# Attention and mixture of experts on one core: a chunk's residual put off by half a slot, and the layernormed inputs of q and k taken amid the next scores

## The chip, the cores and the metric

The kernel runs on one core of a Trainium2 chip. The metric is the device time of the whole program in microseconds (us), shorter is better. A core has a matrix engine (TensorE, "PE"), a vector engine (VectorE, "DVE"), a scalar engine for activation functions (ScalarE, "ACT"), a general one (GpSimd, "POOL") and an engine that issues transfers (SyncE, "SP"). Each works through its own list of instructions, and semaphores order them against each other. Matrix products land in PSUM, an accumulator memory; everything else lives in SBUF, the memory on the core, or in DRAM.

## The reference

The input x has 8 batches of 1024 tokens with 512 features, in 32 bit floating point. Two sublayers follow each other, each with a layernorm before it and a residual sum around it.

```
h   = layernorm(x)
q, k: cos and sin (by a table of 2048 steps) of  h / (1+|w|) + b + t * phi      # t: the token's place
v   = cos + sin of                               h / (1+|w_v|) + b_v
out = softmax(causal(q k^T / sqrt(2*32))) v        # 16 heads of 32 features
x   = x + (cos + sin of out / (1+|w_out|) + b_out)
h   = layernorm(x)
p   = softmax(h Wr + br);  the two best of 8 experts; at most 160 tokens of a batch per expert
x   = x + sum over the two of  p * (relu(h W1[e] + b1[e]) W2[e] + b2[e])
```

The angle formulas work on 16 heads of 32 features. The experts have 2048 hidden features.

## The kernel before, in words

**Slots.** The 512 features of a batch are cut into 4 chunks of 128 features (4 heads). One chunk of one batch is a *slot*, so there are 32 slots, n = 0 to 31, with b, c = divmod(n, 4). The main loop (L1209 on) does one slot per turn, and each turn mixes work of several chunks: scores and value products of chunk n, the rest of the value products and the output of chunk n-1, the angles of chunk n+1 and n+2, and the router of the batch before. After the loop come the experts (`experts`), which the change leaves alone.

**A slot in two halves.** A chunk's four heads make two pairs. `scores` (L584) yields one step at a time. A step multiplies keys with queries for a block of at most 512 queries (L602, with a causal mask added by L616) into a PSUM tile `ps_s`, and ScalarE takes the exponential (L622). A pair has ten steps. `attend` (L627) multiplies the exponentials with v into a tile `av` (L636), and its last step copies that to SBUF as `av_sb` on VectorE (L644). The first half of a slot has the ten steps of pair 0, and the second those of pair 1. `some(k, gen)` takes k steps of a generator, and `rest(gen)` all that are left. `with_asides(k)` (inside the loop) takes k score steps of pair 0, and after each step one step of every generator in `asides`: `v_pre` (three steps of VectorE work for v), one of batch b+1's `layernorm1` halves in some slots, and in slots with c = 2 the router's choice.

**q and k.** `qk_pre(m)` transposes the layernormed input of chunk m on TensorE (16 matmuls, L202) into one `ps_s` tile, and four VectorE instructions (L495) turn it into angles in `qk_f`, adding a table from `qk_base`. `angle` (L426) shifts these into `qk_r`. ScalarE then squares `qk_f` (L430, in two parts) and takes absolute values of `qk_r` into `qk_c` (L509, in two parts): this is `qk_abs`. In the middle of the next slot `qk_sin` takes both sines, and `qk_post` multiplies (L436) and copies the results by eight transfers each (L527) into the next chunk's two `qk` tiles, from `qk_c` first and from `qk_r` second. `qk_f`, `qk_r`, `qk_c` and `qk_base` exist once each, so `angle` may write `qk_r` only when the transfers out of it have landed. `load_base` fetches the next 1 MB table.

**Output and residual.** In slot n `turn` transposes the values of chunk n-1, divides, and `o_pre` makes the output's angle. After the sine and the square `o_post` (L567) does the residual: a product (L436 on `t_r`), a sum into `x_mid` (L576), and eight statistics for the second layernorm (L579). `x_mid` holds one batch of x; `load_mid` fetches it (2 MB, L374) in the slot with c = 1, when the router has read the old one.

**The router** of batch b-1 (`router`, L688) is a generator that runs through slots of batch b. It starts in the second half of the slot with c = 0 (variable `begin`): statistics, an inverse root, and the first two token tiles normalised (L706) and stored. In the slot with c = 1 it takes eight steps at points called `route_on(1)`: four times `features` (transpose two token tiles into a `ps_s` tile, copy them on VectorE to `xT`, L733, and normalise the next two) and, after each, `sums` (product with the router's weights, L767, and a copy, L772). In the slot with c = 2 `sums` ends and the choice of experts follows (L804 to L835).

**Order.** TensorE, VectorE and ScalarE execute in the order in which this program writes their instructions: a manual schedule (`tc.manual_schedule`). Only the queues of SyncE and GpSimd are ordered by the planner of the framework. The planner also decides which free buffer of a pool a tile gets. `ps_s` has three buffers, `av` two, `t_r` and `o_p` two.

The second half of a slot, before the change, in its core:

```
some(2, *ahead)                    # score steps of pair 1
begin = c == 0 and late            # late: not the first slot
if begin:   rest(residual); route = router(b - 1); next(route)
elif ...:   qk_st = rest(qk_pre(n + 2))
next(residual)                     # product and sum of the residual
angle(*qk_st)                      # unless begin
rest(residual)                     # the eight statistics
route_on(1)                        # c == 1: features, the copy L733
```

Of the kernel before, what the change touches and what calls it, by code (L numbers as in the profile page):

```python
# [73 lines left out]
def preln_attn_moe_kernel(  # L74
# [120 lines left out]
    def two_banks():  # L195
        return ps_sc.tile([P, 2, 512], F32, name="ps_s")

    def by_halves(turned, src):

        for a in range(2):  # L200
            r = slice(a * 64, (a + 1) * 64)
            nc.tensor.transpose(turned[:, a, :], src[r, :], ident[r, r])  # L202
# [222 lines left out]
    def angle(p, r):  # L425
        nc.vector.tensor_scalar(r, p, TURN_SHIFT, None, ALU.logical_shift_left)  # L426

    def square(p):
        f = p.bitcast(U16).rearrange("p (s two) -> p s two", two=2)[:, :, 0]
        nc.scalar.activation(p.bitcast(F32), f, AF.Square, bias=split_c, scale=1.0 / FINE)  # L430

    def sine(r):
        nc.scalar.activation(r.bitcast(F32), r, AF.Sin, scale=STEP_ACT)

    def times(out, f, s):
        nc.vector.scalar_tensor_tensor(out, f.bitcast(F32), LIFT, s, ALU.add, ALU.mult)  # L436
# [34 lines left out]
    def load_base(n):  # L471
        if 1 < n < NCH:
            rest(make_base(n))
            return
        p = qkt.tile([P, 2, S], F32, name="qk_base")
        nc.sync.dma_start(p, base_d[n % NCH])
        bases[n] = p

    def qk_pre(n):

        b, c = divmod(n, NCH)
        base = bases.pop(n)
        p = qkt.tile([P, 2, S], I32, name="qk_f")
        r = qkt.tile([P, 2, S], I32, name="qk_r")
        ps = two_banks()
        for t in range(NTT):
            by_halves(
                ps[:, :, t * 64 : (t + 1) * 64],
                xn_tiles[b][t // 4][:, t % 4, c * P : (c + 1) * P],
            )  # L490

        for i in range(2):
            for a in range(2):
                cols = lambda t: t[:, i, :].rearrange("p (t a q) -> p t a q", a=2, q=64)[:, :, a, :]
                nc.vector.scalar_tensor_tensor(  # L495
                    cols(p), ps[:, a, :].rearrange("p (t q) -> p t q", q=64),
                    inv_qk[:, i * NCH + c : i * NCH + c + 1], cols(base), ALU.mult, ALU.add,
                )
            yield p, r

    def qk_abs(st):

        f, r = st
        for i in range(2):
            square(f[:, i, :])
            yield
        c = qkt.tile([P, 2, S], F32, name="qk_c")
        for i in range(2):
            nc.scalar.activation(c[:, i, :], r[:, i, :], AF.Abs)  # L509
            yield c, f, r  # L510

    def qk_sin(st):
        c, f, r = st
        nc.scalar.activation(c, c, AF.Sin, bias=quarter_c, scale=-STEP_ACT)
        sine(r)

    def qk_post(st):
# [36 lines left out]
    def heads(t):  # L554
        return t.rearrange("p (t a d) -> p t a d", a=HPC, d=DH)

    def v_post(n, st):
        times(v_tiles[n % 2][:, :, :, :DH], heads(st[0]), heads(st[1].bitcast(F32)))
# [89 lines left out]
    def some(count, *gens):  # L648

        for gen in gens:  # L650
            while count and next(gen, 0) is None:
                count -= 1

    def rest(gen):
        got = None
        for got in gen:
            pass
        return got
# [207 lines left out]
    def part(gen):  # L866

        for name in gen:
            if name is not None:
                return  # L870
            yield

    def keep(box, gen):
        for box[0] in gen:
            yield
# [302 lines left out]
    NCK = B * NCH  # L1178
# [6 lines left out]
    qk_st = rest(qk_pre(0))  # L1185
    angle(*qk_st)
    rest(base1)
    mask()
    v_st = rest(v_pre(0))
    qk_st = rest(qk_abs(qk_st))  # L1190
    qk_sin(qk_st)
    pairs = rest(qk_post(qk_st))
    sine(v_st[1])
    square(v_st[0])
# [2 lines left out]
    load_base(1)  # L1197
    last = None
    o_st = route = first_rows = None
    place, angles = [None], iter(())  # L1200
    for n in range(NCK):
        more, late = n + 1 < NCK, last is not None
        b, c = divmod(n, NCH)
        if n == NCK - 1:
            to_inputs.close()
            first_rows = experts_begin()
        pos_n = trig.tile([P, S], F32, name="o_p")
        if late:
            e11, halves1, pos = last  # L1209
        es, halves = [[], []], [[], []]  # L1210

        products = [attend(n, 0, h, es[h], halves[0]) for h in range(2)]
        if late:
            products.insert(0, attend(n - 1, 1, 1, e11, halves1))
        ahead = [scores(pairs[0], h, es[h]) for h in range(2)]
        v_box = [None]
        asides = [keep(v_box, v_pre(n + 1))] if more else [first_rows]
        if b == 0 and c in (1, 2):  # L1220
            asides.append(layernorm1(1, c - 1))
        elif c == 0 and b + 1 < B:
            asides.append(layernorm1(b + 1, 1))
        elif c == 3 and b + 2 < B:
            asides.append(layernorm1(b + 2, 0))
        def route_on(slot):
            if c == slot and route is not None:
                next(route)

        def with_asides(count):  # L1230
            for _ in range(count):
                some(1, *ahead)
                for g in asides:
                    next(g, None)


        if late:
            some(3, *products)
        route_on(1)
        route_on(2)  # L1240
        if c == 2 and route is not None:
            asides.append(part(route))
        if n == 0:
            with_asides(3)
            qk_st = rest(qk_pre(1))
            angle(*qk_st)
            angles = keep(place, qk_abs(qk_st))
            with_asides(2)
        else:
            with_asides(5)  # L1250
        route_on(1)
        route_on(1)
        rest(angles)
        if more:
            v_st = v_box[0]
            square(v_st[0])
        if late:
            some(4, *products)
        route_on(1)
        with_asides(5)  # L1260
        for g in asides:
            rest(g)
        if n == 1:
            load_mid(0)
        if late:
            turn(1, halves1, pos)
            o_st = o_pre(n - 1, pos)
        route_on(1)
        if c == 1 and b > 0:
            load_mid(b)  # L1270
        if n == 2:
            load_b1()
        if c == 2 and b + 2 < B:
            load_x(b + 2)
        if c == 3 and b > 0:
            next(route)
            if b > 1:
                fetch_slots(b - 2)
            scatter()


        some(3, *products)
        if more:
            qk_st = place[0]
            qk_sin(qk_st)
            sine(v_st[1])
        if late:
            sine(o_st[1])
        if more:
            post = qk_post(qk_st)  # L1290
            next(post)
        some(NTT, *products)
        if n == 0:
            load_base(2)


        es, halves1 = [[], []], []
        ahead = [scores(pairs[1], h, es[h]) for h in range(2)]
        route_on(1)
        route_on(2)  # L1300
        some(2, *ahead)
        turn(0, halves[0], pos_n)
        next_pairs = rest(post) if more else None
        some(1, *ahead)
        if late:
            square(o_st[0])
            residual = o_post(n - 1, o_st)
        some(2, *ahead)
        begin = c == 0 and late
        if begin:  # L1310

            rest(residual)
            route = router(b - 1)
            next(route)
        elif n + 2 < NCK:
            qk_st = rest(qk_pre(n + 2))
        if late:
            next(residual, None)
        if n + 2 < NCK and not begin:
            angle(*qk_st)  # L1320
        if late:
            rest(residual)
        route_on(1)
        if more and not begin:
            v_post(n + 1, v_st)
        some(3, attend(n, 1, 0, es[0], halves1))
        route_on(1)
        some(5, *ahead)
        if n + 2 < NCK:
            if begin:  # L1330
                qk_st = rest(qk_pre(n + 2))
                angle(*qk_st)
            angles = keep(place, qk_abs(qk_st))
            if not begin:
                some(2, angles)
        if more and begin:
            v_post(n + 1, v_st)
        if n + 3 < NCK:
            load_base(n + 3)
        last = (es[1], halves1, pos_n)  # L1340
        pairs = next_pairs
    rest(attend(NCK - 1, 1, 1, es[1], halves1))
# [54 lines left out]
```

## Time and profile before

| what | value |
|---|---|
| time, median of 3 runs | 3413.85 us (3410.76 to 3418.34) |
| the profiled execution's own time | 3403.52 us |
| span of that execution's profile | 3401.6 us |
| mean granted TensorE clock | 0.982 |
| TensorE busy | 3205.5 us (94%) |
| VectorE busy | 2285.9 us (67%) |
| ScalarE busy | 1320.5 us (39%) |
| first score matmul | 51.85 us |
| slot 17 (batch 4, chunk 1), first score matmul to that of slot 18 | 747.70 to 805.52 us |
| slot 18 (batch 4, chunk 2) | 805.52 to 841.75 us |

The span runs from the first to the last instruction; what lies around it makes the execution's own time. A line of the timeline has the start in us from the span's start, the duration, the engine, the line of the program, the operation, the tiles written and read, their sizes, how many instructions were merged, and in brackets how long the engine was idle just before and who ended that wait. A line of the waits has who waited, for whom, the sum of the waits, how often, and the longest. A wait is put down to the engine whose signal came last.

### The profile page before, as it was taken

How to read it: one execution, taken by the hardware profiler on the slowest of the kernel's cores; microseconds unless marked ns; L12 is line 12 of the kernel's file. 1: busy time of each engine (PE TensorE's matmuls, PEld its weight loads, DVE VectorE, ACT ScalarE, POOL GpSimd, SP SyncE). 2: the span in 40 equal slices, each digit the busy share in tenths (PEclk: the TensorE clock that was granted, in tenths of full speed). 3: DMA queues.
4: the chain of work that ended last, by engine and by line, in shares of the span. 5: the costliest groups of instructions: out<-in, count | busy, mean ns of one | idle time of the engine just before them, and what ended most of it. 6: DMA issues, size and time to landing. Idle time of an engine off the chain costs nothing.

```text
span 3401.6 us, 48876 instructions
## 1 busy us (share of the span) xinstructions
PE 3205.5 (94%) x18942; PEld 2173.0 (64%) x18942; DVE 2285.9 (67%) x5064; ACT 1320.5 (39%) x1609; POOL 417.8 (12%) x363
## 2 busy tenths in 40 slices
PE   3998989898989898899999999999999999999998
PEld 1444444444444444468778778788688688688687
DVE  7886868686868676656566656756747746845844
ACT  5787878787868786311111111101101101201201
POOL 1000202020202021330100110111011011011010
PEclk9999999999999999999999999999999999999999
DMA  4444444444444344232312322322313322323221
GB/s 145 141 123 135 124 137 113 137 119 131 137 137 119 106 132 106 75 97 65 106 50 65 106 48 68 105 44 72 106 38 78 105 36 76 108 43 87 88 41 25
DMA packets 233967, 320.79 MB, mean 94 GB/s; under 512 B 21528, under 2 KB 154376, under 8 KB 221320
## 3 DMA queue, kind: packets, MB, share of 16 engines
q1 hardware_dynamic: 211120, 275.47, 27.6%
q0 software_dynamic: 22528, 42.18, 7.0%
q8 instruction: 150, 2.46, 0.3%
q14 instruction: 81, 0.66, 0.1%
q10 hardware_dynamic: 88, 0.02, 0.0%
HBM read 188.67 MB, written 61.82 MB: 74 GB/s over the span
## 4 chain that ended last, share of the span: by engine, by line
PE 57%; DVE 3%; DMA 1%; issue 1%; ACT 0%; POOL 0%; POOLq 0%; SPq 0%; DVEq 0%; ACTq 0%
PE ps_p L1070 28%; PE ps_p L1025 25%; PE av L636 1%; PE ps_s L602 1%; PE ps_t L981 1%; DMA slot_d<-token,slot 0%; DMA xn_d<-xn 0%; DMA out_dram<-y,slots 0%; DMA xg<-xn_d,source 0%; DMA qk<-qk_r 0%; DVE t L1010 0%; DVE t L1009 0%; ACT hid L1057 0%; DVE hid L1053 0%; DVE y L1086 0%
## 5 line engine op out<-in xcount | busy, mean ns | idle before, releaser
L622 ACT ACTIVATE e<-ps_s 128x1024 f32<-128x1024 f32 (+1 forms) x640 | 569.3, 937 | 299.2 <-PE ps_s L602 202.8
L602 PE MATMUL ps_s<-qk 64*128 64x512 f32 (+3 forms) x3072 | 605.7, 513 | 55.4 <-DMA qk<-qk_r 21.4
L1070 PE MATMUL ps_p<-w,hid 128*128 128x256 f32 x2560 | 569.9, 380 | 0.0
L1070 PEld LDWEIGHTS ps_p<-w,hid 128*128 128x128 f32 x2560 | 485.3, 191 | 65.8
L636 PE MATMUL av<-e,v 128*64 128x512 f32 (+3 forms) x3072 | 524.4, 491 | 0.0
L1070 PE MATMUL ps_p<-w_t,hid 128*128 128x256 f32 x1920 | 430.0, 379 | 0.0
L602 PEld LDWEIGHTS ps_s<-qk 64*128 64x128 f32 x3072 | 267.2, 191 | 246.9 <-issue 154.6
L1070 PEld LDWEIGHTS ps_p<-w_t,hid 128*128 128x128 f32 x1920 | 362.4, 190 | 47.2
L636 PEld LDWEIGHTS av<-e,v 128*64 128x64 f32 x3072 | 200.5, 137 | 284.0 <-issue 265.6
L1025 PE MATMUL ps_p<-xe_s,t 128*128 128x256 f32 (+1 forms) x1024 | 297.8, 434 | 5.8 <-DVE t L1010 3.4
L1025 PE MATMUL ps_p<-xe,w 128*128 128x256 f32 (+1 forms) x1024 | 300.9, 437 | 1.4 <-DVE o_p L673 1.2
L684 POOL DMA_INDIRECT slot_d<-token,slot x128 | 163.9, 1281 | 1093.2 <-issue 561.3
L1025 PE MATMUL ps_p<-xe,t 128*128 128x256 f32 (+1 forms) x1024 | 296.9, 433 | 0.0
L1099 ACT COPY p<-ps_p 128x256 f32<-128x256 f32 x40 | 14.7, 368 | 613.0 <-PE ps_p L1070 613.0
L1025 PEld LDWEIGHTS ps_p<-xe_s,t 128*128 128x128 f32 x1024 | 194.0, 190 | 90.0 <-DVE t L1010 7.9
L1025 PEld LDWEIGHTS ps_p<-xe,w 128*128 128x128 f32 x1024 | 194.2, 191 | 84.3 <-DVE hid L1043 6.0
L1025 PEld LDWEIGHTS ps_p<-xe,t 128*128 128x128 f32 x1024 | 194.6, 190 | 80.7 <-issue 0.4
L1092 POOL DMA_INDIRECT out_dram<-y,slots x80 | 126.2, 1578 | 667.5 <-DVE y L1087 527.2
L964 POOL DMA_INDIRECT xg<-xn_d,source x80 | 78.2, 978 | 1053.8 <-PE ps_t L981 1022.7
L1040 ACT ACTIVATE p<-ps_p,b_t 128x256 f32<-128x256 f32 (+1 forms) x128 | 65.4, 511 | 329.7 <-DVE y L1086 169.7
L1044 ACT ACTIVATE hid<-hid 128x256 f32<-128x256 f32 (+1 forms) x128 | 60.1, 470 | 324.6 <-DVE hid L1043 324.6
L1057 ACT ACTIVATE hid<-hid,b_more 128x256 f32<-128x256 f32 (+1 forms) x128 | 71.8, 561 | 270.1 <-DVE hid L1056 270.1
(210 smaller groups left out, 3840.2 us busy)
## 6 DMA issues: line engine op xcount, KB each, us to landing
w<-in_L_ffn_W_dram SPq DMA_DIRECT2D x256, 256.0 KB, 3.3
qk<-qk_c SPq DMA_DIRECT2D x128, 256.0 KB, 4.4
qk<-qk_r SPq DMA_DIRECT2D x128, 256.0 KB, 3.9
w<-in_L_ffn_W_dram SPq DMA_DIRECT2D x64, 512.0 KB, 7.0
qk_base<-base_d SPq DMA_DIRECT2D x29, 1024.0 KB, 7.1
xn_d<-xn SPq DMA_DIRECT2D x72, 256.0 KB, 4.0
x_mid<-in_L_attn_x_dram SPq DMA_DIRECT2D x16, 1024.0 KB, 10.1
out_dram<-x_mid SPq DMA_DIRECT2D x8, 2048.0 KB
```

Of the source, the lines that this page charges most:

```text
L602: nc.tensor.matmul(ps[:, a, at : at + w], lhsT=pair[r, 1, kb * P : (kb + 1) * P], rhs=pair[r, 0, q0 : q0 + w], start=at == 0, stop=not own ...
L622: nc.scalar.activation(e, ps[:, :, :n], AF.Exp, scale=UNIT * UNIT / math.sqrt(2 * DH))
L636: nc.tensor.matmul(av[a * 64 : (a + 1) * 64, q0 - 512 * h :], lhsT=vt[:, kb, 2 * pr + a, :], rhs=es[i][:, a, at : at + w], start=kb == 0, ...
L684: nc.gpsimd.indirect_dma_start(out=slot_d[b], out_offset=bass.IndirectOffsetOnAxis(ap=idx, axis=0), in_=src, in_offset=None,)
L964: nc.gpsimd.indirect_dma_start(out=xg, out_offset=None, in_=xn2_d[i % 2], in_offset=bass.IndirectOffsetOnAxis(ap=source[:, e, j0 + j, None ...
L981: nc.tensor.transpose(ps[:, c, :], xg[:, c * P : (c + 1) * P], ident)
L1025: nc.tensor.matmul(ps, lhsT=weights[:, k, :], rhs=rows[:, k, :], start=k == 0, stop=k == 1)
L1040: nc.scalar.activation(p1, product(b11, a11), AF.Identity, bias=b1_t[:, e * NHC + q : e * NHC + q + 1])
L1044: nc.scalar.activation(h11, h11, AF.Relu)
L1057: nc.scalar.activation(h12, h12, AF.Relu, bias=more)
L1070: nc.tensor.matmul(ps, lhsT=hs[k][:, part, cols], rhs=ws[k][weight], start=k == 0, stop=k == NHQ - 1,)
L1092: nc.gpsimd.indirect_dma_start(out=out, out_offset=bass.IndirectOffsetOnAxis(ap=meta[:, e, jj[r], 0:1], axis=0), in_=ys[r], in_offset=None ...
```

## The change

Four things move; no operation is added or removed.

1. In the slot with c = 1 the residual (that of the batch's chunk 0) no longer runs in the second half. It runs in the next slot, c = 2, in the first half after two score steps.
2. In the slots with `begin` (c = 0, n = 4, 8, ... 28) `qk_pre(n+2)`, its `angle` and `load_base(n+3)` no longer stand at the slot's end. They run in the next slot, c = 1, in the first half after two score steps. The multiplication `v_post` in these slots moves up to where the other slots have it.
3. In slot 0 `qk_pre(1)` and its `angle` come after two score steps in place of three.
4. Ahead of the loop ScalarE takes the absolute values and the first sine before the two squares, in place of after them. To allow this, `qk_abs` is split into `squares` and `absolutes`, and `both` does the two in the old order.

```diff
-    def qk_abs(st):
-
-        f, r = st
+
+    def squares(f):
         for i in range(2):
             square(f[:, i, :])
             yield
+
+    def absolutes(st):
+        f, r = st
         c = qkt.tile([P, 2, S], F32, name="qk_c")
         for i in range(2):
             nc.scalar.activation(c[:, i, :], r[:, i, :], AF.Abs)
             yield c, f, r
 
-    def qk_sin(st):
+    def both(st):
+        yield from squares(st[0])
+        yield from absolutes(st)
+
+    def qk_sin(st, between=()):
         c, f, r = st
         nc.scalar.activation(c, c, AF.Sin, bias=quarter_c, scale=-STEP_ACT)
+        for _ in between:
+            pass
         sine(r)
...
-    qk_st = rest(qk_abs(qk_st))
-    qk_sin(qk_st)
+    qk_st = rest(absolutes(qk_st))
+    qk_sin(qk_st, squares(qk_st[1]))
...
+    begin = False
-    place, angles = [None], iter(())
+    place, angles, residual = [None], iter(()), iter(())
...
-        if n == 0:
-            with_asides(3)
-            qk_st = rest(qk_pre(1))
+        with_asides(2)
+        if n == 0 or begin:
+
+            qk_st = rest(qk_pre(n + 1))
             angle(*qk_st)
-            angles = keep(place, qk_abs(qk_st))
-            with_asides(2)
-        else:
-            with_asides(5)
+            angles = keep(place, both(qk_st))
+            if begin:
+                load_base(n + 2)
+        with_asides(3)
+        rest(residual)
         route_on(1)
         route_on(1)
...
-        if late:
+
+        if c != 1:
             next(residual, None)
         if n + 2 < NCK and not begin:
             angle(*qk_st)
-        if late:
+        if c != 1:
             rest(residual)
         route_on(1)
-        if more and not begin:
+        if more:
             v_post(n + 1, v_st)
         some(3, attend(n, 1, 0, es[0], halves1))
         route_on(1)
         some(5, *ahead)
-        if n + 2 < NCK:
-            if begin:
-                qk_st = rest(qk_pre(n + 2))
-                angle(*qk_st)
-            angles = keep(place, qk_abs(qk_st))
-            if not begin:
-                some(2, angles)
-        if more and begin:
-            v_post(n + 1, v_st)
-        if n + 3 < NCK:
-            load_base(n + 3)
+        if n + 2 < NCK and not begin:
+            angles = keep(place, both(qk_st))
+            some(2, angles)
+            if n + 3 < NCK:
+                load_base(n + 3)
```

## The prediction

> **What bounds the kernel now.** I read the page first: the busy shares, then the chain that ended last.
>
> ```profile
> PE 3205.5 (94%) x18942; PEld 2173.0 (64%) x18942; DVE 2285.9 (67%) x5064; ACT 1320.5 (39%) x1609; POOL 417.8 (12%) x363
> PE 57%; DVE 3%; DMA 1%; issue 1%; ACT 0%; POOL 0%; POOLq 0%; SPq 0%; DVEq 0%; ACTq 0%
> ```
>
> TensorE is the bound, so an edit is worth what it does to TensorE's idle time, slot by slot. I cut the attention half at every 96th score matmul (L602), which gives its 32 slots, and summed TensorE's idle time in each. From slot 3 on, slots of chunk 0, 2 and 3 idle 0.0 to 0.2 us (the last slot apart). Slots of chunk 1 (5, 9, ... 29) idle about 3.3 us in their first half and 10.0 to 12.5 us in the second; they last 56.7 to 59.3 us, the others 36. The view of waits names the causes:
>
> ```profile
> PE ps_s L767 <- DVE xT L733: 74.8, 7, 12.3
> DVE qk_r L426 <- DMA qk<-qk_r: 63.2, 23, 6.3
> PE ps_s L602 <- DVE xT L733: 11.8, 7, 1.7
> PE ps_s L602 <- DVE qk_f L495: 10.5, 8, 1.5
> ```
>
> The first row, 74.8/7 = 10.7 us a slot, is the prize: the router's sums wait for a copy by VectorE. The last two are the 3.3 us of the first half. Slot 17 stands for the seven. TensorE's timeline, first half and then second:
>
> ```profile
> 750.35 1.14 PE L602 MATMUL ps_s<-qk 64*128 64x384 f32 x8 [1.48 <-DVE qk_f L495]
> 753.85 1.99 PE L602 MATMUL ps_s<-qk 64*128 64x512 f32 x8 [1.68 <-DVE xT L733]
> ...
> 795.10 1.08 PE L767 MATMUL ps_s<-xT,wr_sb 128*32 128x256 f32 x8 [10.58 <-DVE xT L733]
> 796.11 4.82 PE L602 MATMUL ps_s<-qk 64*128 64x512 f32 x12
> ```
>
> VectorE in the same stretch (start, duration):
>
> ```profile
> 785.27 1.23 DVE L576 SCALAR_TENSOR_TENSOR x_mid<-t_r,x_mid 128x1024 f32<-128x1024 f32 x1
> 791.08 1.23 DVE L426 TENSOR_SCALAR qk_r<-qk_f 128x2048 int32<-128x2048 int32 x1 [4.59 <-DMA qk<-qk_r]
> 792.22 1.64 DVE L579 BATCH_NORM_STATS2 st_mid<-x_mid 128x6 f32<-128x128 f32 x8
> 793.78 1.27 DVE L733 COPY xT<-ps_s 128x512 f32<-128x512 f32 x2
> ```
>
> So the copy is last in a row: the residual's two products, then `angle` (L426), idle 4.59 us until the copies out of the previous `qk_r` have landed, then the residual's eight statistics, then the copy. Only the statistics stand between that landing and the copy. SyncE's issues show why it lands late:
>
> ```profile
> 771.54 1.07 SPq L374 DMA_DIRECT2D x_mid<-in_L_attn_x_dram  x2
> 773.91 2.42 SPq L527 DMA_DIRECT2D qk<-qk_c  x4
> 781.30 3.27 SPq L527 DMA_DIRECT2D qk<-qk_r  x4
> 784.67 1.54 SPq L476 DMA_DIRECT2D qk_base<-base_d  x1
> ```
>
> With 2 MB of `x_mid` and 1 MB each of `qk_c`, `qk_r` and the base table, the DMA share is 1.00 to 1.06 in each 3 us from 774 to 789.
>
> **What the Trainium skill says.** (1) PSUM — Partial Sum Buffer, "Engine vs sequencer instructions": VectorE's queue is strictly first in, first out. The trace agrees: the copy's transposes end at 781.98, but it runs at 793.78, behind `angle`. (2) Trainium Kernel Development and Optimization, "Key Constraints": transfers from all queues share the same 16 DMA engines; the share of 1.0 fits. (3) TensorE: Matmul & The Clock Gate, "What's actually happening": after an idle window of about 3.4 us the clock halves, and comes back after a busy one, on a free-running grid. Here the granted clock is 0.50 from 789 to 798, and twelve score matmuls take 4.82 us at 796.11 against 2.85 in the next slot (813.22). (4) Perfetto Trace Analysis, "Optimization Strategy": a repeating gap on the saturated engine can mean too few PSUM buffers; the 1.48 and 1.68 us above are such waits for one of the three `ps_s` tiles.
>
> **The change part by part**, on slot 17's clock.
>
> *Residual out of chunk 1's second half* (8 batches, of which 7 have a router). Its ten VectorE instructions go: 1.22 + 1.23 + 1.64 us. The first two end at 786.50, inside the wait for the landing (791.08), so they yield nothing: the wait just grows to 7 us. The statistics yield 793.78 - 792.22 = 1.56 us. `angle` keeps its place ahead of the copy, and I find nothing that would make the landing earlier: the same transfers are issued in the same order. TensorE then resumes near 793.5, still after more than 8 us idle, so the half clock stays; where its grid falls is chance (per slot, half of up to 3.4 us). Sum: 7 x 1.56 = **-10.9 us**.
>
> *Residual into chunk 2's first half, after two score steps.* It adds 4.05 us of VectorE between `v_pre`'s second and third part. Queued behind: the `t_r` shift (ScalarE's square of v waits), the router's choice (3.6 us of small operations), `av_sb` (TensorE's `turn` waits). From slot 18's rows: the shift moves from 808.59 to 812.6 and ends at 813.3, where ScalarE's square began at 813.16; the choice's idle 0.32 us is absorbed and `av_sb`, 813.33 to 814.08, ends at 817.6. The `turn` that reads it:
>
> ```profile
> 813.33 0.75 DVE L644 TENSOR_SCALAR av_sb<-av,inv_o 128x512 f32<-128x512 f32 x1 [0.17 <-PE av L636]
> 817.59 0.66 PE L202 MATMUL ps_s<-ident,av_sb 64*128 64x64 f32 x16
> ```
>
> Its first eight transposes read the other half, so the need is at 817.9: hidden, with 0.3 us to spare; **0**. If that cover were gone, each us late costs 7. Later on VectorE idles 1.70 us at 826 and has caught up. In batch 0 (slot 2) there is no router but layernorm1 of batch 1, and VectorE has no idle time from 138.06 to 160. It starts 1.2 us ahead, then loses 4.05: `av_sb` (151.54, 0.75) ends near 155.0, against a need at 152.9. **+2.2 us**, once.
>
> *q/k inputs moved from the end of chunk 0 to chunk 1, after two score steps* (7 times: 16 transposes, four L495 of together 2.72 us, `angle` 1.23, a 1 MB base load). The two waits above (3.2 us) lose their cause, and TensorE could start the 20 value matmuls (756.98) at about 754.8, 2.2 us earlier. But VectorE is busy without a break from 734.70 to 761.5 with the same work in another order: the next router copy (758.26, 1.28) still ends near 759.5, the next sums begin there (before: 760.29), and `angle` now ends at 757.3 (rows 0,1 end at 746.91; then `v_post` 1.22, `av_sb` 0.74, copy 1.28, rows 1.1, v 1.28 + 1.23, L495 2.72, `angle` 1.23, less 0.08 overlap each). Behind it waits ScalarE, and behind that the next five exponentials:
>
> ```profile
> 756.91 2.19 ACT L430 ACTIVATE qk_f<-qk_f,split_c 128x1024 f32<-128x1024 uint16 x2
> 762.07 4.39 ACT L622 ACTIVATE e<-ps_s 128x1024 f32<-128x1024 f32 x5
> ```
>
> They come 0.4 us later than now, and features(2) already waited 0.16 us for one of them. So I take no gain here, a loss of 0.4 us at most, and that falls into the 9 us wait for the DMAs, whose head (`x_mid`, 771.54) hangs on VectorE's chain and stays. **0**; bounds -2.2 (all gained) and +3.0 (below). The base load goes on SyncE behind two stores of rows (754.40) to about 756; it takes 7 us and is read at 781: hidden. `v_post` at chunk 0 comes earlier; `av_sb` behind it is read some 17 us later: 0.
>
> *Start.* Squares behind absolute values and the first sine: the four operations end at 40.6 in any order, and their reader began at 41.31 behind v's shift: 0. In slot 0 the inputs come one score step (0.6 us) earlier; a wait of 4.86 us hangs on their `angle`: **-0.6**.
>
> Sum: -10.9 + 2.2 - 0.6 = **-9.3 us**. On the profiled execution, 3403.5 us (span 3401.6), this gives 3394.2. That execution lies 10 us below the median of the three runs, so I carry the difference over: 3413.85 - 9.3, rounded **3405**.
>
> **Rivals.** *Boundary gain too*: ScalarE or VectorE is less tight than I read, and the whole first half, head of the DMAs included, moves 2.2 us up. For it: the waits of 22 us in the table do vanish. Against: VectorE's unbroken row. 7 x (-1.56 - 2.2) + 1.6 = -24.7: 3389. *The transfer eats it*: `qk_r` lands later by what the statistics free, or `av_sb` in chunk 2 is 1.5 us late. For it: DMA at its limit, cover of only 0.3 us. Against: unchanged order of issues. 1.6 + about 0: 3415. *Slower, by a PSUM buffer*: the inputs' transposes hold one of three `ps_s` tiles until VectorE reads them at 753.5 to 756.2. If the third score step is given that tile, it waits from 750.3 to 756.2; steps 3 to 5 (2.5), sums (0.6) and features (0.7) put the value matmuls at 760.0, +3.0 us, and the DMAs' head with them: 7 x (3.0 - 1.56) + 1.6 = +11.7: 3425.5. For it: today the second step after the inputs got just that tile (1.48 us). Against: the third then took the one freed by an exponential. It decides once the tile's reuse delays the slot by over 1.5 us.
>
> **How the numbers follow.** Chances: forecast 0.55, boundary gain 0.12, transfer 0.16, PSUM 0.17. Within 0.2% (6.8 us, about what a measurement of this kernel can tell) is 3407.0 to 3420.7. The forecast's own range is 3400 to 3411: 1.0 to 1.9 us a slot, 1 to 3 in slot 2, the clock's grid, and the runs' own spread (3410.8 to 3418.3). Two thirds of it, 0.37, is faster and 0.18 the same. Faster 0.37 + 0.12 = 0.49; same 0.18 + 0.16 = 0.34; slower 0.17. Leaving out half of the PSUM case and most of the boundary case, the range is 3391 to 3425.
>
> **What the new profile would show.** Right: L767 waits about 9 us seven times (63 to 65 in all), with the copy directly behind `angle`, whose wait for the DMA is near 7 us; the two rows of 11.8 and 10.5 gone; slot 2 with 2 us idle before `turn`. Wrong: a new wait of L602 for L495 inside chunk 1's first five steps; `turn` in chunk 2 waiting for `av_sb`; or `angle` beginning at another distance from the first `x_mid` issue than today's 19.5 us.

## The result, and the profile after

| what | before | after |
|---|---|---|
| time, median of 4 runs | 3412.31 us (3407.37 to 3418.34) | 3438.27 us (3433.42 to 3442.92) |
| ratio after to before | | 1.0075, 95% interval 1.0053 to 1.0097 |
| profiled execution's own time | 3403.52 us | 3437.18 us |
| span of that execution | 3401.6 us | 3435.3 us |
| mean granted TensorE clock | 0.982 | 0.977 |

The change makes the kernel slower by 0.5 to 1.0%. The prediction was 3405 us, with a range up to 3425: wrong in sign and outside its range.

One slip stands in the text on record, in the section on the change and in the prediction alike. They put the moved residual of chunk 2 "after two score steps". In the code it stands behind `with_asides(2)`, the q/k inputs and `with_asides(3)`: behind all **five** score steps, and so behind the router's choice. Only the q/k inputs come after two.

The line numbers of after are 8 higher than those of before from `scores` on (L602 is L610, L706 is L714, L733 is L741, L767 is L775).

The page of after has this busy time of each engine.

```profile
PE 3229.5 (94%) x18942; PEld 2178.0 (63%) x18942; DVE 2285.3 (67%) x5064; ACT 1323.7 (39%) x1609; POOL 418.4 (12%) x363
```

The same 18942 matmuls keep TensorE busy for 24.0 us more: part of them ran at the lower clock. VectorE's busy time is the same to 0.6 us.

I cut the loop at every 96th score matmul, as before, and compared the slots of the two profiled executions:

| part | before, us | after, us | difference |
|---|---|---|---|
| up to the first score matmul | 51.85 | 52.05 | +0.2 |
| slots 0 and 1 | 88.66 | 89.15 | +0.5 |
| chunk 0 with a router (7 slots) | 255.03 | 253.70 | -1.3 |
| chunk 1 with a router (7 slots), first halves | 193.1 | 226.2 | **+33.1** |
| the same, second halves | 211.2 | 198.4 | **-12.8** |
| slot 2 (batch 0, chunk 2) | 36.37 | 39.82 | +3.45 |
| slot 30 (batch 7, chunk 2) | 35.74 | 40.16 | +4.4 |
| chunk 2, the other 6 slots | 217.43 | 218.29 | +0.9 |
| chunk 3 and last slot | 298.13 | 298.28 | +0.15 |
| behind the loop | 2014.1 | 2019.2 | +5.1 |

So the expected gain in the second halves came, and the first halves of the same slots took it back more than twice over. The 5.1 us behind the loop are not laid to the change: over the experiments below that stretch lies between 2012.9 and 2017.7 us with no relation to what was edited. In after it is still 1.5 us longer than in any of them; why stays open.

The view of waits of after:

```profile
PE ps_s L775 <- DVE xT L741: 69.3, 14, 10.0
DVE qk_r L426 <- DMA qk<-qk_r: 82.4, 23, 7.9
DVE xn L714 <- DMA xn_d<-xn: 23.0, 10, 3.7
PE ps_s L758 <- DVE lg L780: 19.9, 7, 3.7
```

The first row has 14 waits now instead of 7; seven new, short ones stand in the first halves. The second grew from 63.2 to 82.4 us: `angle` in the second half waits longer for the same landing, as predicted. The last two are new in size. Before, the row of `xn` had 4.9 us in 5 waits; now VectorE waits 23.0 us until earlier rows have been stored, 20.05 of it in the seven first halves (before, 0.91, all of it in slot 21). And TensorE waits 19.9 us for a router copy of VectorE.

Slot 17 again, first half (it starts at 755.69, 8.0 us later than before). VectorE, after:

```profile
757.05 1.27 DVE L741 COPY xT<-ps_s 128x512 f32<-128x512 f32 x2
761.53 1.00 DVE L714 TENSOR_SCALAR xn<-x_mid,mv,rstd 128x512 f32<-128x512 f32 x2 [3.21 <-DMA xn_d<-xn]
...
764.91 2.72 DVE L495 SCALAR_TENSOR_TENSOR qk_f<-ps_s,inv_qk,qk_base 128x512 int32<-128x512 f32 x4
767.67 1.23 DVE L426 TENSOR_SCALAR qk_r<-qk_f 128x2048 int32<-128x2048 int32 x1
...
769.58 0.41 DVE L780 COPY lg<-ps_s 128x256 f32<-128x256 f32 x1
769.91 1.27 DVE L741 COPY xT<-ps_s 128x512 f32<-128x512 f32 x2
```

SyncE's issues, after:

```profile
749.59 1.10 SPq L701 DMA_DIRECT2D out_dram<-x_mid  x1
754.91 8.00 SPq L720 DMA_DIRECT2D xn_d<-xn  x4
```

The router keeps the normalised rows in two buffers (`xn2`). `rows(0)` and `rows(1)` fill them, SyncE stores them to DRAM, and `rows(2)` and `rows(3)` may overwrite them only when these stores have landed. Ahead of them in the queue lies the 2 MB store of `x_mid`. The stores of rows 0 and 1 were issued from 754.91 on, and VectorE could write again at 761.53: 6.6 us. It came for the buffers at 761.53 - 3.21 = 758.32, 3.4 us after the issue, and so it stood. Before, it came much later. SyncE, then VectorE, before:

```profile
741.11 1.11 SPq L693 DMA_DIRECT2D out_dram<-x_mid  x1
746.48 1.98 SPq L712 DMA_DIRECT2D xn_d<-xn  x2
```

```profile
753.71 1.11 DVE L706 TENSOR_SCALAR xn<-x_mid,mv,rstd 128x512 f32<-128x512 f32 x2
```

Issued at 746.48, wanted at 753.71: 7.2 us, of which `av_sb`, the four L495, `angle`, `v_post` and the copy filled the time. Four L495 (2.72) and `angle` (1.23) are exactly what the change took out of this place. They were the cover of the stores. Some 0.6 us were to spare (7.2 against the 6.6 measured in after). Before itself agrees: in its slot 25 the store of row tile 1, issued at 1081.10, landed 6.6 us later, 0.6 us before its buffer was written again.

Behind the waiting `rows(2)` in VectorE's list stand v's two products, L495, `angle`, the shift and both router copies. TensorE, after:

```profile
763.46 3.23 PE L644 MATMUL av<-e,v 128*64 128x512 f32 x20
770.04 0.31 PE L758 MATMUL ps_s<-gather_e,lg 128*32 128x8 f32 x16 [3.35 <-DVE lg L780]
771.23 1.08 PE L775 MATMUL ps_s<-xT,wr_sb 128*32 128x256 f32 x8 [0.88 <-DVE xT L741]
772.24 5.28 PE L610 MATMUL ps_s<-qk 64*128 64x512 f32 x12
```

TensorE stands for 4.2 us between the value matmuls and the sums, and then twelve score matmuls take 5.28 us, where the same kind of row took 2.85 elsewhere. The answer by windows (stretch, its length, then busy us of PE, PEld, DVE, ACT and POOL, granted clock, DMA share, GB/s) has the reason:

```profile
766.70:770.00 3.30, 0.00 (x0) 0.00 (x0) 3.27 (x6) 1.07 (x2) 1.75 (x2) 1.00 0.32 20
772.00:775.00 3.00, 3.00 (x12) 1.22 (x10) 1.16 (x4) 2.62 (x4) 0.00 (x0) 0.50 0.90 298
```

First TensorE has nothing to do for 3.3 us while VectorE is busy for all of it; then it works at half clock. The Trainium skill, TensorE: Matmul & The Clock Gate, "What's actually happening", has a free-running window of 3413 ns after which an idle array falls to half clock. The trace agrees on the window: stretches of half clock in the loop have lengths of 3.4, 6.8, 10.2 or 13.7 us, and within a trace they begin on one grid of 3.41 us. On "idle" the measurement differs. In the window ahead of this stretch (766.89 to 770.30) TensorE worked 0.26 us, and in slot 2 of after a window with 1.58 us of work (152.49 to 155.91) was followed by half clock all the same. Over the nine traces, from 60 us on and but for the last 20, every such window at full clock with less than 1.5 us of TensorE's busy time (whose ends the profile models) was followed by half clock, and none with more than 1.8: the boundary lies near half a window of work.

The sum of the seven first halves: idle time of TensorE 23.3 us before and 35.9 after, +12.6; 30.3 us of its work at half clock, of which half, 15, is loss (an estimate: full clock would take half the time); the 16 transposes that the inputs bring along, 7 x 0.55 = 3.9. Together 31.5 of the 33.1 us.

### The profile page after: what moved, and what is told of

The parts are those of the page before. It is cut to its first block, busy times and chain, and to the rows that moved or that the text cites. A ratio compares the mean times of both kernels' runs of the same rounds, so it can differ in the third digit from the quotient of the medians.

```text
span 3435.3 us, 48869 instructions
## 1 busy us (share of the span) xinstructions
PE 3229.5 (94%) x18942; PEld 2178.0 (63%) x18942; DVE 2285.3 (67%) x5064; ACT 1323.7 (39%) x1609; POOL 418.4 (12%) x363
## 3 DMA queue, kind: packets, MB, share of 16 engines
q1 hardware_dynamic: 211120, 275.47, 27.6%
## 4 chain that ended last, share of the span: by engine, by line
PE 56%; DMA 2%; DVE 1%; issue 1%; POOL 0%; ACT 0%; SPq 0%; POOLq 0%; DVEq 0%; ACTq 0%
PE ps_p L1078 28%; PE ps_p L1033 26%; DMA slot_d<-token,slot 2%; PE ps_t L989 1%; PE av L644 0%; PE ps_s L610 0%; DMA out_dram<-y,slots 0%; DMA xg<-xn_d,source 0%; DMA qk<-qk_r 0%; DVE y L1094 0%; ACT e L630 0%; POOL slot_d L692 0%; DVE t L1018 0%; DVE u L1120 0%; DVE t L1017 0%
## 5 line engine op out<-in xcount | busy, mean ns | idle before, releaser
L610 PE MATMUL ps_s<-qk 64*128 64x512 f32 (+3 forms) x3072 | 616.3, 521 | 33.6 <-DMA qk<-qk_r 21.5
L610 PEld LDWEIGHTS ps_s<-qk 64*128 64x128 f32 x3072 | 269.3, 194 | 234.3 <-issue 148.6
L1033 PE MATMUL ps_p<-xe_s,t 128*128 128x256 f32 (+1 forms) x1024 | 300.6, 437 | 10.2 <-POOL t L1018 6.8
```

The lines of the kernel that those rows point to most:

```text
L610: nc.tensor.matmul(ps[:, a, at : at + w], lhsT=pair[r, 1, kb * P : (kb + 1) * P], rhs=pair[r, 0, q0 : q0 + w], start=at == 0, stop=not own ...
L1033: nc.tensor.matmul(ps, lhsT=weights[:, k, :], rhs=rows[:, k, :], start=k == 0, stop=k == 1)
```

## The experiments

All ratios are to the kernel before, run on the same chip: 3406.16 us for the first set (15 runs), 3405.85 for the second (25 runs). No kernel leaves out anything of the reference.

**The residual alone.** The kernel before, with nothing but the first of the four moves.

```diff
...
+        rest(residual)          # behind the five score steps of pair 0
         route_on(1)
...
-        if late:
+        if c != 1:
             next(residual, None)
...
-        if late:
+        if c != 1:
             rest(residual)
```

> The kernel before with only the residual of a batch's first chunk moved (out of chunk 1's second half, to behind chunk 2's first five score steps, as the changed kernel has it). Theory A (the loss sits in the moved q/k inputs: behind the earlier router copy VectorE waits for the stores of the first two row tiles): no wait for row stores; each of seven slots of chunk 1 gains about 1.6 us, slots 2 and 30 lose some 8 us together as in the changed kernel; about 3409, between 3402 and 3414. Theory B (the residual's new place is what costs): 3425 or more.

3403.75 us (3398.98 to 3408.85), ratio 0.9991 (0.9981 to 1.0001). First halves of the seven slots 192.7 us, as before; second halves 201.1, or 10.1 less. Its view of waits has the router's wait shortened by just the statistics, from 74.8 to 64.0:

```profile
PE ps_s L767 <- DVE xT L733: 64.0, 7, 10.2
```

Little of it is left at the end: slot 2 takes 1.8 us more, slot 30 4.2 and the other chunk-2 slots 0.9. So the residual's move is not what slowed the kernel. That it makes it faster is not shown, since the interval touches 1.

**The inputs of q and k, and the start, without the residual.** The kernel after, with the residual where it was.

```diff
         with_asides(3)
-        rest(residual)
         route_on(1)
...
-        if c != 1:
-            next(residual, None)
+        next(residual, None)
...
-        if c != 1:
-            rest(residual)
+        rest(residual)
```

> The changed kernel with the residual where it was before; the q/k inputs, slot 0 and the start as changed. Theory A: the first halves of chunk 1 are as long as in the changed kernel (29.4 to 34.4 us) with VectorE waiting 1 to 4 us for row stores, the second halves keep the 1.6 us that the residual's move saves, slots 2 and 30 are as before: about 3438 + 11 - 8 = 3441, between 3433 and 3449. Theory B: below 3420.

3434.24 us (3428.76 to 3445.24), ratio 1.0089 (1.0068 to 1.0110). First halves 221.2 us, second 211.6 as before, and the wait for the stores is there:

```profile
DVE xn L714 <- DMA xn_d<-xn: 21.5, 10, 2.7
```

So the loss comes with the move of the inputs (and of the `v_post` that goes with it) and does not need the residual's move; that it is not the start's shows in the place, slots 5 to 29. With the residual's move the first halves take 5.0 us more (226.2), 4.6 of it by the half clock.

**The 2 MB store behind the first rows.** If the stores of the rows land late because `x_mid` leaves ahead of them, issuing that store after them should bring the buffers back in time. The kernel after, with one line moved in `router`:

```diff
-        nc.sync.dma_start(token_tiles(out[b * S : (b + 1) * S, :]), xt)
         mv = small.tile(...)
...
         ahead = [rows(0), rows(1)]
+        nc.sync.dma_start(token_tiles(out[b * S : (b + 1) * S, :]), xt)
         yield "tiles"
```

> The changed kernel; only the 2 MB store of x_mid to the output is issued behind the stores of the router's first two row tiles in place of ahead of them. Theory A (the row stores land late because they queue behind that store): VectorE's wait for row stores falls from 23 us in total to under 4, the two gaps of TensorE at the router's second sums (20 us and some 6 us) to under 8 together, half the half-clock time in the first halves goes; the seven first halves lose about 29 us: near 3410, between 3403 and 3418. Rival C (the 3.95 us of moved q/k work itself stand ahead of the second router copy and cost the slot): VectorE's wait goes but the slots stay over 30 us; 3425 or more.

3427.56 us (3421.95 to 3432.26), ratio 1.0055 (1.0037 to 1.0074): some 17 us short of what I expected. The waits (the lines behind the moved one are 1 lower than in after):

```profile
DVE xn L713 <- DMA xn_d<-xn: 5.0, 8, 1.2
PE ps_s L774 <- DVE qk_f L495: 19.6, 6, 4.6
```

The wait for the stores fell from 23.0 to 5.0 us, so the 2 MB store ahead made most of it. But another wait took its place. The first `sums` were now given the `ps_s` tile that the inputs' transposes had filled, and had to wait until L495 had read it; in after no sums wait for L495. TensorE's half-clock work in the first halves was 32.0 us (30.3 in after), and they took 216.0. This is the mechanism of the prediction's slower rival, at another instruction and only in this variant: a planner that hands out buffers anew after each edit can turn one wait into another. By its time alone the run falls into rival C's range, since here too the moved inputs cost the slot; it does not decide between the two theories, and the next run does.

**Rows behind v's products.** To mend the wait without touching the transfers, the second pair of rows is put off until VectorE has done v's two products, just ahead of the inputs. The kernel after, and:

```diff
+    put_off = []
...
-            if g + 1 < NTT // 2:
+            if g == 0 and not last:
+                put_off.append(lambda: ahead.extend([rows(2), rows(3)]))
+                del ahead[:]
+            elif g + 1 < NTT // 2:
                 ahead[:] = [rows(2 * g + 2), rows(2 * g + 3)]
...
         with_asides(2)
+        while put_off:
+            put_off.pop()()
         if n == 0 or begin:
```

> The changed kernel; in chunk 1 of the batches with a router, normalising row tiles 2 and 3 (which has to wait for the stores of tiles 0 and 1) stands behind the two products for v, 2.5 us later, still ahead of the moved q/k inputs. Theory A (that wait, 1.2 to 3.7 us a slot, delays everything behind it on VectorE, and the gap it makes halves TensorE's clock): the wait falls below 1 us in each slot, the first halves of the seven slots lose 12 to 22 us together; about 3420, between 3413 and 3428. Rival C (the moved q/k work itself is what costs, whatever waits ahead of it): no gain over 5 us, 3431 or more.

3411.0 us (3402.84 to 3422.95), ratio 1.0015 (1.0007 to 1.0024), lower than the range I had given. First halves 202.6 us, 23.6 less than after. VectorE and TensorE in slot 17 (lines up to 5 higher than in after):

```profile
752.95 1.23 DVE L716 TENSOR_SCALAR xn<-x_mid,mv,rstd 128x512 f32<-128x512 f32 x2
...
759.06 0.31 PE L763 MATMUL ps_s<-gather_e,lg 128*32 128x8 f32 x16 [0.28 <-DVE lg L785]
```

The rows wait only 0.14 us in this slot and TensorE stands 0.28 us at the sums, where it stood 3.35. In the first halves the clock does not fall, except in slot 21, where rows 2 and 3 still wait 3.8 us, against the expectation of under 1: batch 4 stores each row twice. Rival C is out: the moved work is all there, and the first halves lost 23.6 us. So 1.2 us of VectorE's work, put 2.5 us later in its list, won back most of the loss: 25.8 us between the profiled executions (3435.3 and 3409.5 us), some 20 us by the two ratios. What remains over before is in slots 21 and 25 (+4.2 and +1.8), slots 2 and 30 (+3.5 and +4.2) and the stretch behind the loop (2017.7 against 2014.1), against -11.1 in the second halves.

**`angle` behind the router's copies.** The prediction said that in the second half the copy is late because `angle`, ahead of it in VectorE's list, waits for a landing. If so, `angle` behind the copy is worth more than the residual. The kernel before, and:

```diff
-        if n + 2 < NCK and not begin:
+        if n + 2 < NCK and not begin and not (c == 1 and b):
             angle(*qk_st)
...
         route_on(1)
+        if n + 2 < NCK and c == 1 and b:
+            angle(*qk_st)
         some(5, *ahead)
```

> The kernel before with one edit: in slots of chunk 1 with a router, the shift of the q/k angles (which waits for the copies out of the old qk_r) stands behind the router's last copies of the half, in place of ahead of its fourth copy. If that wait for the DMA is what makes the sums wait 10.7 us, L767 waits about 3.5 us in place of 10.7 and the clock no longer halves: 7 x (7 + 2) us less, about 3350, between 3340 and 3365. If TensorE is then held by something else of the same length (the exponentials' buffers, the next slot's squares), it stays over 3390.

3365.72 us (3363.92 to 3367.57), ratio 0.9879 (0.9862 to 0.9895); the time lies just past the end of the range. The router's wait:

```profile
PE ps_s L767 <- DVE xT L733: 34.2, 7, 4.9
```

Of 10.7 us a slot 4.9 are left: now the copy waits behind the residual's products and statistics. The expectation had 3.5 and no half clock, and missed both: each second half still has 3.4 or 6.8 us of half clock. The second halves take 168.8 us (211.2 before); 40.5 of these 42.4 us are TensorE's idle time.

**Both: residual and `angle` out of the way.** The kernel before with the last edit, and the residual put off for batches 1 to 6 alone, since slots 2 and 30 have no room for it:

```diff
...
+        rest(residual)
...
-        if late:
+        if c != 1 or b in (0, B - 1):
             next(residual, None)
```

> The kernel before with the angle's shift behind the router's copies (as in the run that had this alone, 3366) and the residual moved as in the changed kernel, but for batches 1 to 6 alone; the q/k inputs stay where they were before. If VectorE's order is what is left of the router's gap, L767 waits under 1.5 us in slots 5 to 25 in place of 4.88, and the residual costs nothing in chunk 2: 6 x (4 + 1.5) less than that run, about 3335, between 3325 and 3350. If the gap is held by something else, it stays at 3360 or more.

3332.64 us (3328.64 to 3336.54), ratio 0.9778 (0.9765 to 0.9792), as expected, and faster than both kernels. In slot 17:

```profile
751.14 1.28 DVE L733 COPY xT<-ps_s 128x512 f32<-128x512 f32 x2
752.47 0.64 PE L767 MATMUL ps_s<-xT,wr_sb 128*32 128x256 f32 x8 [0.82 <-DVE xT L733]
...
758.05 1.23 DVE L426 TENSOR_SCALAR qk_r<-qk_f 128x2048 int32<-128x2048 int32 x1 [3.42 <-DMA qk<-qk_r]
```

`angle` still waits for its landing, but here nobody queues behind it. The sums wait 0.82 us, the slot takes 45.6 us (57.8 before), and slots 5 to 25 have no half clock at all; slot 29, whose residual was left in place, still has 6.8 us. Chunk 2 did not stay free of cost as expected: its six other slots take 5.6 us more than before, 4.0 of it in slot 22, where `angle` waits 6.38 us at the head and ScalarE's work, TensorE and the clock follow. Alone, the residual's move took 10.1 us from seven second halves; here, in six slots, it gave 3365.72 - 3332.64 = 33 us. Ahead of a waiting `angle` its two products lay inside that wait and only the statistics counted; without the wait all of it lies ahead of the copy. In the second halves TensorE's idle time falls by 24.4 us, which is six times the residual's 4.1; the half clock that goes with it gives another 11.9.

**The same with the inputs moved.** The kernel after with the edits of the last three (rows put off, `angle` behind the copies, residual of batches 0 and 7 left): does the move of the inputs pay once its wait is mended?

```diff
-        if c != 1:
+        if c != 1 or b in (0, B - 1):
             next(residual, None)
...
-        if n + 2 < NCK and not begin:
+        if n + 2 < NCK and not begin and not (c == 1 and b):
             angle(*qk_st)
...
```

> The changed kernel with the residual of batches 0 and 7 left where it was, row tiles 2 and 3 behind the products for v, and the angle's shift behind the router's copies: the q/k inputs stay in chunk 1. Theory A: with its wait gone, the input move costs nothing or gains up to 2 us a slot against the run without it: 3320 to 3340. Rival C: it costs 2 us or more a slot, 3350 or more.

3341.76 us (3338.1 to 3344.22), ratio 0.9812 (0.9797 to 0.9827), between what the two theories said. First halves of chunk 1 202.6 us against 193.1, of which 3.9 us are the transposes, which chunk 0 no longer has (-3.2 us there). The rest, 5.6 us, is mostly slots 21 and 25, where rows still wait for stores. The kernel without the move of the inputs (and of the start) is 9 us faster in the medians, and the intervals of the two ratios don't meet, so these moves don't pay even then. (The two profiled executions, 3336.54 and 3338.1 us, are the slowest of the one and the fastest of the other.) The waits of L602 that it removes (22 us in the first view of waits) bought nothing here.

## Why the prediction was wrong

**The step that failed** is "q/k inputs moved from the end of chunk 0 to chunk 1 ... 0; bounds -2.2 and +3.0". Its working lists VectorE's instructions behind each other, "copy 1.28, rows 1.1, v", as if each could start when the one before ended. The rows could not: they need two buffers whose stores land 6.6 us after their issue, and the inputs that the step moved away were what VectorE did meanwhile. The price is 33.1 us in seven first halves, 4.7 a slot, above the upper bound of 3.0. The durations in the row were right: where the rows don't wait (slot 17 with the rows put off) the stretch from the end of rows 0 and 1 to the end of `angle` takes 10.7 us, against 10.4 in the prediction (10.2, if 0.08 is taken off for each of its eight parts). With the wait gone the forecast of 0 nearly holds: the first halves other than slots 21 and 25 take 28.0 to 28.5 us against 27.5 to 27.6, and 0.55 of that are the transposes. The kernel's code shows the two buffers and the store in `rows`, and in before VectorE already waited 0.91 us for them in slot 21, so there the cover was used up. Of the moved step I had asked what it would delay in its new place, and not what it had been hiding in its old one. The kernels with the residual alone and with all but the residual put the loss on this step; the rows put off show the mechanism, since the wait and the half clock go together, and 23.6 us of the 33.1 come back.

**Residual out of chunk 1**: right. Predicted -1.56 us a slot, measured -12.8/7 = -1.83 in after and -10.1/7 = -1.44 with the residual alone; the router's wait of 64.0 us with the residual alone lay in the forecast's 63 to 65, and in after `angle` waited 7.11 us in slot 17.

**Residual in chunk 2**: the result was right (0.14 us a slot), the working not, since it was made for two score steps and the residual runs behind five. Slot 2 was to cost 2.2 us and cost 1.83 alone and 3.45 in after, where half of a half-clock stretch of 3.4 us comes on top. Slot 30 was missed, +4.4 us: TensorE stands 2.70 us there for `av_sb`, about as much as VectorE's instructions ahead of it are longer than elsewhere (2.8 us, last section), and half of such a stretch comes on top here too.

**Start**: -0.6 predicted, +0.7 measured up to slot 2. Kernels that leave this part as it was differ by as much, so the runs don't decide it.

**The rivals.** The boundary gain did not come, not even with the rows put off: VectorE's row was the limit, as argued. The waits of L602 for L495 and for the copy did vanish from chunk 1. The slower case had 0.17 and the right sign, by another mechanism: in after no score step of chunk 1 waits for L495, so the right sign was luck. Its own mechanism appeared when the store was moved. Its price, 3.0 us a slot, held only the delay of the value matmuls and not the clock, whose share of the loss (15 us) is larger than that of the new idle time (12.6).

## What to carry to other kernels

Before moving work away from a place, look for what finishes behind it: take each transfer issued shortly before, add the time to its landing, and find the next instruction that writes its buffer; if that one now comes earlier than the landing, the move buys a wait for everything queued behind it. A wait on an in-order engine hides what stands ahead of it, so ask first what the needed instruction is queued behind (here `angle`, worth 40 us) and only then shorten the work around it, which may count for little alone and for 33 us afterwards. On TensorE a new wait of some 4 us can cost as much again by the clock, and in slot 2 of after a wait of 1.84 us was enough for a stretch at half clock.

## What the runs showed of the hardware

VectorE's and GpSimd's instructions on SBUF tensors can stretch each other. In slot 30, GpSimd mixes weights for the first expert while the router's choice and the moved residual run. In the timeline of after:

```profile
1334.12 0.22 DVE L829 SCALAR_TENSOR_TENSOR tmp<-tmp,e_row 128x64 f32<-128x64 f32 x1
1335.64 0.73 POOL L1018 TENSOR_TENSOR t<-w,t 128x256 f32<-128x256 f32 x1
1336.49 0.77 DVE L829 SCALAR_TENSOR_TENSOR tmp<-tmp,e_row 128x64 f32<-128x64 f32 x1
1338.13 1.77 DVE L436 SCALAR_TENSOR_TENSOR t_r<-o_p,t_r 128x1024 f32<-128x1024 f32 x1
1338.78 1.71 POOL L1018 TENSOR_TENSOR t<-w,t 128x256 f32<-128x256 f32 x1
1339.93 1.63 DVE L584 SCALAR_TENSOR_TENSOR x_mid<-t_r,x_mid 128x1024 f32<-128x1024 f32 x1
```

The same router instruction takes 0.22 us as GpSimd starts (1334.26) and 0.77 beside it; the residual's product takes 1.77 instead of 1.22 and its sum 1.63; and GpSimd's own product goes from 0.73 to 1.71. Ahead of `av_sb` the lengthenings of VectorE add up to 2.8 us. The Trainium skill, SBUF — State Buffer, "SBUF: two separate sides", says that the two engines share a pair of ports, which one instruction holds for its whole length; VectorE's instructions with two SBUF inputs are among those that need it beside a GpSimd instruction that reads SBUF. The durations fit. All that grew have two SBUF inputs, while a reduction with one (L827, at 1335.80) keeps its 0.22 us amid GpSimd's product. The ends fit taking turns, as far as GpSimd's spans can be trusted: GpSimd's product ends 0.59 us after VectorE's (1339.90 to 1340.49), and VectorE's sum 1.07 us after that (1341.56), each about its length when alone (0.73 and 1.22). No run here takes GpSimd's work out of that slot, so the cause is argued from the overlap alone.
